# Loads of the attention layers, moved from SyncE's DMA queue to ScalarE's

## The chip, the core and the metric

The kernel runs on one core of a Trainium2 chip. The metric is the device time of one execution in microseconds (us). PE is TensorE (PEld its weight loads), DVE is VectorE, ACT is ScalarE, POOL is GpSimd and SP is SyncE. Besides computing, an engine can start DMAs: a DMA stands in the engine's instruction order like any other instruction, waits there for what it needs, is issued, and then runs on the core's 16 DMA engines by itself. SP does nothing else.

## The reference

Four graph layers over 2708 nodes with 512 features, all with the same symmetric 0/1 adjacency matrix of about 0.6% ones. Layer 2 is the one that matters here: two attention layers in a row, the second with a residual and a layer norm behind it.

```python
def _gat_layer(x, W, adj):
    proj = x @ W
    Wh, Ws = jnp.split(proj, 2, axis=-1)
    scores = Wh @ Ws.T
    a = jax.nn.softmax(scores, axis=-1) * adj
    out = a @ Wh
    out = out + x
    return jax.nn.leaky_relu(out, NEG_SLOPE)

x = _layernorm(x + _L0_gnn_ref(x, adj, deg[..., None], L0_gnn_W, L0_gnn_b), axis=-1)
x = _layernorm(x + _L1_gnn_ref(x, adj, L1_gnn_W, L1_gnn_b), axis=-1)
x = _layernorm(x + _L2_gnn_ref(x, adj, L2_gnn_W_stack), axis=-1)   # two _gat_layer
x = _layernorm(x + _L3_gnn_ref(x, adj, L3_gnn_W, L3_gnn_b), axis=-1)
```

The softmax is over all nodes, and the mask comes after it, so that every score is needed for the divisors while only the neighbours' values are summed.

## The kernel before

The nodes are cut into 22 blocks of 128 rows and, as columns, into six chunks `CH` of 512, 512, 512, 512, 384 and 276. Layers 0, 1 and 3 multiply the adjacency matrix, loaded as bytes or floats and cast by ACT to tiles `m`, into `acc` (`acc<-m,xh` and `acc<-m,xl`). The class `Attention` does the two attention layers, numbers 0 and 1.

For each attention layer the weights are first mixed (`mix`), then for each chunk the stationary side of the scores (`wst_sb`) and the values `z` are projected, and sums of quarters of the stationary side (`s1`, `s2`, `s4`, the stationary sums) are made. `keep_sums` stores these sums to DRAM, and `load_sums` brings them back when a later chunk needs them. `copy_z` copies the values into a DRAM table `pairs`.

`layer` walks over the chunks. For chunk `k` the scores of all 22 blocks against the chunk's columns are made on PE:

- `load_moving` loads the turned rows of the chunk (`xs`, four tiles), at block 15 of the chunk before.
- In chunks 0 to 3 of layer 0 and 0 to 2 of layer 1 (`SEVEN`), `pair_steps` makes two blocks at a time in seven products instead of eight: PE writes banks `spx` and `spy`, ACT copies them at once to tiles `s`, `u` and `v`, and PE adds the next product onto the same bank. In the other chunks `scores` makes each block from four products into a bank `sp`.
- `soften`, one chunk behind, takes a block of the finished chunk: DVE subtracts the column's maximum, ACT takes the exponential, DVE adds it to the divisor's sum and multiplies it by the mask `a`, and SP stores it to `pairs` (`pairs<-s`).
- `fetch`, once the whole chunk is stored, gathers the neighbours' rows of a block from `pairs` by an indirect DMA on POOL (`g<-pairs,givers`). With it come the residual rows `xr` of this and the next block (`load_rows`), and in layer 1 the first inputs `x1` (named `x<-x` in the profile).
- `weigh` multiplies the gathered rows on PE (`acc<-g`), and `end` adds the residual rows, applies the leaky relu and stores the block (`y<-r`, or after the layer norm `x<-r`).

Between these, `fill` puts in work of the next layer: the second attention layer's projections, and layer 3's first products.

The order is set by hand. The wrapper `Ordered` makes each engine run its instructions in the order of the calls:

```python
if engine in last:
    self.owner.tc.add_manual_dep(ins.ins, last[engine], ...)
last[engine] = ins.ins.name
```

`advance` keeps an estimated clock by which gathers and later steps are placed. All SBUF tiles of 2 KB a partition come from one pool of 87 pages (`page`), and a page is taken again when its last user is done. There are eight PSUM banks, in two pools of four (`bank`).

Before the change all of the loads named above, the masks and the stores stand in SP's queue; POOL's queue has the gathers and other transfers of layers 0, 1 and 3. ACT starts no DMA in the part that runs (a general path, taken for other weights only, follows it).

Of the kernel before, what the change touches and what calls it, by code (L numbers as in the profile page):

```python
# [552 lines left out]
class Fast:  # L553
# [266 lines left out]
    def load_rows(self, ly, j):  # L820
        if ly.rows[j] is None:
            ly.rows[j] = self.page(f"x{ly.number}_{j}")
            queue = self.nc.gpsimd if ly.number == 1 else self.nc.sync
            queue.dma_start(ly.rows[j], ly.source[j])
# [807 lines left out]
class Attention:  # L1632
# [414 lines left out]
    def load_sums(self, ly, k):  # L2047

        for n, name in enumerate(("s1", "s2", "s4")):
            t = self.page(f"{name}_{ly.number}_{k}", FP, (P, 2, 2 * P))  # L2050
            self.nc.sync.dma_start(t, self.sums[ly.number][k][n])
            ly.sums[k][name] = [t[:, c, :] for c in range(2)]

    def replace(self, ly, k):
# [145 lines left out]
    def load_moving(self, ch):  # L2200

        ch.xt = []
        for c in range(DC):
            t = self.page(f"xs{ch.name}_{c}")
            self.nc.sync.dma_start(
                t[:, : ch.cw], self.k.turned[ch.ly.number][ch.k][:, c, :]
            )
            ch.xt.append(t)
# [155 lines left out]
    def fetch(self, ch):  # L2364


        q, t = ch.to_fetch.pop(0)
        g = self.f.wide(f"g{ch.name}_{q}_{t}")
        i, _, w = ch.blocks[q]

        for b in (q, q + 1):
            self.load_rows(ch, b)
        if ch.ly.number == 1 and q not in ch.first:
            ch.first[q] = self.page(f"x1{ch.name}_{q}")
            self.nc.sync.dma_start(ch.first[q][:w], self.k.saved[1][i][:w])

        h = t // ONLY if t < QUARTERS * ONLY else (0, QUARTERS - 1)[q % 2]
        first, width = (P, D + (h + 1) * QW) if q % 2 else (h * QW, D + P - h * QW)
        self.nc.gpsimd.indirect_dma_start(
            out=g[:, :width],  # L2380
            out_offset=None,
            in_=ch.ly.pairs[ch.k % 2][:, :],
            in_offset=bass.IndirectOffsetOnAxis(ap=self.k.givers[:, i, t : t + 1], axis=0),
            element_offset=(q // 2) * PAIR + first,
        )

        begin = max(self.fetch_free, self.clock + (FIRST_LANDS if (q, t) == ch.first_fetch else 0))
        self.fetch_free = begin + 1.15
        ch.fetched.append((g, self.fetch_free + 6))

    def load_rows(self, ch, q):
        if q in ch.rows or q >= len(ch.blocks):
            return
        ch.rows.add(q)
        i, _, w = ch.blocks[q]
        ch.x[q] = self.page(f"xr{ch.name}_{q}")
        given = self.k.saved[1] if ch.ly.number == 0 else self.k.between
        self.nc.sync.dma_start(ch.x[q][:w], given[i][:w])

    def fetch_ahead(self):  # L2400
        count = sum(len(c.fetched) for c in self.chunks)
# [331 lines left out]
```

## Time and profile before

| | |
|---|---|
| Time, median of 3 runs | 2238.84 us |
| Lowest and highest | 2234.57 and 2247.07 us |
| The profiled execution | 2238.97 us |
| Its span, first to last instruction | 2236.7 us |
| Granted TensorE clock | 0.992 |
| First attention layer's scores | from about 735 us |
| Second attention layer's scores | from about 1420 us |
| DMA moved | 487.90 MB, 218 GB/s on average |
| SP's and POOL's queues | 36.5% and 29.3% of 16 DMA engines' span |

The profile is that of one execution. "Busy" leaves out waits, semaphores and the issue of DMAs. Rows of groups read: line, engine, operation, output<-inputs, shape, count, and then busy time or durations. Line 71 is the wrapper through which every operation is issued, so the tile names tell groups apart. In a timeline a row gives start, length, engine and operation, and in brackets how long the engine stood idle before it and what seems to have released it; "issue" means that the profile shows nothing it waited for, and "remote" an unknown queue. A wait for several things is put down to the one that came last. SPq is SP's sequencer, which issues DMAs. Times on a timeline count from the span's start.

### The profile page before, as it was taken

How to read it: one execution, taken by the hardware profiler on the slowest of the kernel's cores; microseconds unless marked ns; L12 is line 12 of the kernel's file. 1: busy time of each engine (PE TensorE's matmuls, PEld its weight loads, DVE VectorE, ACT ScalarE, POOL GpSimd, SP SyncE). 2: the span in 40 equal slices, each digit the busy share in tenths (PEclk: the TensorE clock that was granted, in tenths of full speed). 3: DMA queues.
4: the chain of work that ended last, by engine and by line, in shares of the span. 5: the costliest groups of instructions: out<-in, count | busy, mean ns of one | idle time of the engine just before them, and what ended most of it. 6: DMA issues, size and time to landing. Idle time of an engine off the chain costs nothing.

```text
span 2236.7 us, 30610 instructions
## 1 busy us (share of the span) xinstructions
PE 2182.9 (98%) x10012; PEld 1576.6 (70%) x10012; DVE 1626.8 (73%) x3425; ACT 824.9 (37%) x1855; POOL 722.2 (32%) x827
## 2 busy tenths in 40 slices
PE   9999999999999999999999999999999998999997
PEld 6777788889887888765555666788743455577896
DVE  6777888897887869987758733459979698545744
ACT  7444363333333345433323422335423223342121
POOL 2333441111000000657465452000466666643000
PEclk9999999999999999999999999999999999999999
DMA  9976762222412855999799885674899899974221
GB/s 347 287 199 171 197 189 65 88 84 91 158 58 96 289 176 155 318 327 333 244 357 342 277 287 178 212 259 134 274 324 322 284 329 354 324 242 129 94 87 43
DMA packets 310990, 487.90 MB, mean 218 GB/s; under 512 B 37434, under 2 KB 178010, under 8 KB 310820
## 3 DMA queue, kind: packets, MB, share of 16 engines
q1 hardware_dynamic: 242164, 270.69, 36.5%
q0 software_dynamic: 68656, 215.15, 29.3%
q8 instruction: 81, 1.33, 0.2%
q14 instruction: 89, 0.73, 0.1%
HBM read 356.23 MB, written 162.76 MB: 232 GB/s over the span
## 4 chain that ended last, share of the span: by engine, by line
PE 94%; DVE 2%; issue 1%; DMA 1%; another core or an unknown queue 1%; ACT 0%; DVEq 0%; ACTq 0%; POOL 0%; POOLq 0%
PE acc L71 39%; PE sp L71 13%; PE spx L71 10%; PE spy L71 7%; PE mm L71 4%; PE mmx L71 3%; PE mmy L71 2%; PE z_0x L71 2%; PE wst L71 2%; PE z_0y L71 1%; PE mix L71 1%; PE wst_0x L71 1%; PE wst_1x L71 1%; PE z_1x L71 1%; PE wst_0y L71 1%
## 5 line engine op out<-in xcount | busy, mean ns | idle before, releaser
L71 POOL DMA_INDIRECT g<-pairs,givers x510 | 540.1, 1059 | 808.0 <-DMA xr<-x 235.3
L71 PE MATMUL acc<-m,xh 128*128 128x512 f32 (+4 forms) x1584 | 562.1, 376 | 6.7 <-ACT s L71 6.7
L71 PE MATMUL acc<-m,xl 128*128 128x512 f32 (+4 forms) x1584 | 548.1, 364 | 0.3 <-issue 0.3
L71 PEld LDWEIGHTS acc<-m,xh 128*128 128x128 f32 (+1 forms) x1584 | 287.4, 188 | 64.3 <-issue 17.2
L71 PEld LDWEIGHTS acc<-m,xl 128*128 128x128 f32 (+1 forms) x1584 | 287.7, 188 | 42.4 <-issue 3.6
L71 PE MATMUL sp<-xs,wst_sb 128*128 128x384 f32 (+2 forms) x960 | 301.5, 486 | 0.1
L71 PE MATMUL acc<-g 128*32 128x512 f32 (+1 forms) x1020 | 273.1, 613 | 7.2 <-issue 4.1
L71 PEld LDWEIGHTS sp<-xs,wst_sb 128*128 128x128 f32 x960 | 166.4, 183 | 133.0 <-issue 74.4
L71 ACT CAST m<-at 128x512 fp32r<-128x512 uint8 (+5 forms) x396 | 201.8, 569 | 111.4 <-DMA at<-mask 47.9
L71 DVE TENSOR_TENSOR sum<-sum,s 128x512 f32<-128x512 f32 (+4 forms) x252 | 156.9, 623 | 30.2 <-ACT s L71 22.9
L71 DVE TENSOR_TENSOR s<-s,a 128x512 f32<-128x512 f32 (+3 forms) x264 | 166.1, 629 | 9.1
L71 PEld LDWEIGHTS acc<-g 128*32 128x32 f32 (+1 forms) x1020 | 77.9, 136 | 134.4 <-issue 105.9
L71 DVE TENSOR_TENSOR top<-top,s 128x512 f32<-128x512 f32 (+3 forms) x240 | 149.4, 623 | 26.2 <-issue 15.3
L71 DVE TENSOR_TENSOR s<-s,shift 128x512 f32<-128x512 f32 (+3 forms) x264 | 161.2, 619 | 1.6 <-issue 1.3
L71 ACT COPY s<-sp 128x384 f32<-128x384 f32 (+2 forms) x112 | 52.5, 473 | 291.3 <-PE sp L71 153.9
L71 ACT ACTIVATE s<-s 128x512 f32<-128x512 f32 (+3 forms) x264 | 146.8, 581 | 13.5 <-DVE s L71 8.4
L71 POOL DMA_DIRECT2D x<-o x44 | 25.7, 590 | 325.2 <-DVE o L71 281.8
L71 ACT COPY s<-spx 128x256 f32<-128x256 f32 x210 | 77.5, 373 | 136.7 <-PE spx L71 98.1
L71 PE MATMUL spx<-xs,wst_sb 128*128 128x256 f32 x400 | 103.2, 383 | 0.0
L71 PE MATMUL mm<-w,ht 128*128 128x512 f32 (+1 forms) x240 | 99.1, 594 | 0.0
L71 DVE SCALAR_TENSOR_TENSOR xr<-acc,rden,xr 128x512 f32<-128x512 f32 (+1 forms) x44 | 32.8, 746 | 84.6 <-PE acc L71 65.2
L71 PEld LDWEIGHTS spx<-xs,wst_sb 128*128 128x128 f32 x400 | 76.0, 191 | 19.5 <-issue 7.4
(349 smaller groups left out, 3331.0 us busy)
## 6 DMA issues: line engine op xcount, KB each, us to landing
pairs<-s SPq DMA_DIRECT2D x168, 256.0 KB
at<-in_adj_t SPq DMA_DIRECT2D x84, 256.0 KB
pairs<-pairs SPq DMA_DIRECT2D x42, 512.0 KB
s<-sums SPq DMA_DIRECT2D x60, 256.0 KB
xres<-x POOLq DMA_DIRECT2D x44, 256.0 KB
x<-o POOLq DMA_DIRECT2D x43, 256.0 KB
pairs<-z_sb SPq DMA_DIRECT2D x42, 256.0 KB
pairs<-pairs SPq DMA_DIRECT2D x42, 256.0 KB
```

The source lines that it names most:

```text
L71: ins = call(*args, **kw)
```

## The change

Four loads are issued by ACT (`nc.scalar`) instead of SP (`nc.sync`), at the same places of the program. In ACT's order they now stand between the copies and exponentials that were called before and after them. There are 60 loads of stationary sums, 40 of turned rows, 44 of residual rows and 22 of first inputs, 166 in all, of mostly 256 KB.

```diff
@@ load_sums
-            self.nc.sync.dma_start(t, self.sums[ly.number][k][n])
+            self.nc.scalar.dma_start(t, self.sums[ly.number][k][n])
@@ load_moving
-            self.nc.sync.dma_start(
+            self.nc.scalar.dma_start(
                 t[:, : ch.cw], self.k.turned[ch.ly.number][ch.k][:, c, :]
             )
@@ fetch
-            self.nc.sync.dma_start(ch.first[q][:w], self.k.saved[1][i][:w])
+            self.nc.scalar.dma_start(ch.first[q][:w], self.k.saved[1][i][:w])
@@ load_rows
-        self.nc.sync.dma_start(ch.x[q][:w], given[i][:w])
+        self.nc.scalar.dma_start(ch.x[q][:w], given[i][:w])
```

The order of PE's, DVE's and POOL's instructions stays the same, and so does that of the DMAs that are left on SP.

## The prediction

> **What bounds the kernel now.** I read the page first (busy shares and the chain that ended last):
>
> ```profile
> PE 2182.9 (98%) x10012; PEld 1576.6 (70%) x10012; DVE 1626.8 (73%) x3425; ACT 824.9 (37%) x1855; POOL 722.2 (32%) x827
> PE 94%; DVE 2%; issue 1%; DMA 1%; another core or an unknown queue 1%; ACT 0%; DVEq 0%; ACTq 0%; POOL 0%; POOLq 0%
> ```
>
> TensorE is the bound: idle for 2236.7 - 2182.9 = 53.8 us of the span, and nothing else can be won. Then the windows over the attention stages: chunks 0 to 3 of the first layer, chunks 3 to 5 of the second, and the second layer's end (columns: length, busy of PE, PEld, DVE, ACT, POOL, granted clock, DMA share, GB/s):
>
> ```profile
> 785.00:1065.00 280.00, 267.55 (x1196) 199.01 (x1194) 230.51 (x390) 115.78 (x273) 103.33 (x96) 0.98 0.78 263
> 1640.00:1890.00 250.00, 249.70 (x882) 123.50 (x881) 209.26 (x384) 78.65 (x152) 161.04 (x150) 1.00 0.94 315
> 1890.00:2005.00 115.00, 104.62 (x417) 65.90 (x416) 61.37 (x139) 49.47 (x99) 61.15 (x62) 0.97 0.88 296
> ```
>
> PE loses 12.5 us in the first and 10.4 us in the last, almost none between, where DMA is busiest. ScalarE is idle for over half of each: it has time, and what counts is when it stands still. So the timelines, first where ScalarE (ACT) paused, then the PE instruction behind it, with PE's idle time in brackets:
>
> ```profile
> 939.29 0.37 ACT L71 COPY v<-spx 128x256 f32<-128x256 f32 x1 [9.28 <-PE spx L71]
> 939.71 1.13 PE L71 MATMUL spx<-t,wst_sb 128*128 128x256 f32 x4 [0.83 <-issue]
> 955.68 0.37 ACT L71 COPY s<-spx 128x256 f32<-128x256 f32 x1 [6.96 <-remote]
> 957.60 2.07 PE L71 MATMUL spx<-t,wst_sb 128*128 128x256 f32 x4 [3.95 <-ACT v L71]
> 1062.88 0.37 ACT L71 COPY v<-spx 128x256 f32<-128x256 f32 x1 [7.39 <-issue]
> 1063.31 2.07 PE L71 MATMUL spx<-t,wst_sb 128*128 128x256 f32 x4 [4.88 <-issue]
> 1602.31 0.37 ACT L71 COPY v<-spx 128x256 f32<-128x256 f32 x1 [6.46 <-DMA pairs<-s]
> 1602.73 1.13 PE L71 MATMUL spx<-t,wst_sb 128*128 128x256 f32 x4 [0.90 <-ACT v L71]
> 1630.58 0.37 ACT L71 COPY s<-spy 128x256 f32<-128x256 f32 x1 [10.51 <-DMA pairs<-s]
> 1631.01 2.07 PE L71 MATMUL spy<-xs,wst_sb 128*128 128x256 f32 x4 [4.60 <-issue]
> ```
>
> They give a price: a pause of ScalarE costs PE the pause less 8.45, 3.01, 2.51, 5.56 and 5.91 us. I call that difference the cover; its mean is 5.1 us. Two pauses end on a store `pairs<-s`, which frees the page.
>
> **What the change removes from SP.** The rows by tile give the issues (ns: shortest, median, longest):
>
> ```profile
> L71 SPq DMA_DIRECT2D s<-sums x60: 319/404/3445, 786.2 to 1586.7; - x60
> L71 SPq DMA_DIRECT2D xs<-t x40: 319/446/946, 779.4 to 1819.2; - x40
> L71 SPq DMA_DIRECT2D xr<-x x22: 319/458/3094, 900.9 to 1344.0; - x22
> L71 SPq DMA_DIRECT2D xr<-y x22: 218/454/1049, 1583.0 to 2001.4; - x22
> L71 SPq DMA_DIRECT2D x<-x x34: 5/472/1102, 1584.0 to 2003.2; - x34
> ```
>
> Of `x<-x` only 22 are first inputs. 166 issues leave SP: 60 x 0.404 + 40 x 0.446 + 22 x (0.458 + 0.454 + 0.472) = 72.5 us. Does PE get any of it? SP mostly waits for data:
>
> ```profile
> SPq L71 <- DVE s L71: 300.1, 143, 17.4
> ```
>
> so a load ahead of a store usually delays nothing. One place shows that it can:
>
> ```profile
> 1611.52 2.02 SPq L71 DMA_DIRECT2D xs<-t  x4
> ...
> 1617.71 7.88 SPq L71 DMA_DIRECT2D pairs<-s  x3
> ```
>
> The first of these three stores had its data at 1612.8 (DVE's record) and landed at 1630.48, ending the pause of 10.51 us. With the loads gone it could go 4.9 us earlier, and the 4.60 us that PE stood go with it. I take 3 of them. Bounds: nothing, and 15.2 us if all five PE pauses above (0.83 + 3.95 + 4.88 + 0.90 + 4.60) vanish. I stay near the low end, since only two of the five name a store.
>
> [...]
>
> **What it adds to ScalarE: issue.** The same 72.5 us, if ACT needs what SP needs. No row shows ACT issuing a DMA; from the SP rows the ends are 0.32 us (53 us in all) and a stall of 3.4 us in a few of them; the median is the nearest row. Three loads take 1.3 us and four 1.8 us, under the smallest cover of 2.51 us: nothing for PE by themselves. With the cover gone, all 72.5 us.
>
> **What it adds: waits.** This is the part that decides. In the built programs every DMA of SP or ACT counts on one of eight counters, used by turns, and is made to wait until the earlier DMA on its counter has landed. On SP such a wait held up DMAs alone. On ScalarE it holds up what is queued behind it: copies that free PSUM banks (PE waits for those) and exponentials (DVE, then the stores, wait for those). For each load I took its place in ACT's order, when ACT came by there, and when the DMA it would wait for landed. At most places that had landed. The others:
>
> A. 921.60, four `xs` and an `xr` behind an exponential. The fifth waits for a store issued at 926.73 and landed at 931.46: 9.86 + 0.45 - 5.1 = 5.2 us.
> B. 942.28, the last of three `sums`: a store landed at 952.87, 10.59 us later. ACT comes 5.2 us later than before, because of A. If the store isn't put off too, 10.59 - 5.2 + 0.45 - 5.1 = 0.7 us; if it is, 5.9 us. I take 3.3.
> C. 1605.83, six loads. The fifth waits for the first, whose landing took 6.13 us: 6.13 + 2 x 0.45 - 5.1 = 1.9 us.
> D. 1620.07, until 1630.48. ACT stood there already until 1630.58: nothing.
> E. 792.11 and 798.15, 3.7 and 4.2 us, while `z` is copied. Below the cover, and SP has 7.9 us fewer loads there by then: nothing.
> F. Chunks 4 and 5 and the layers' ends: 1184.13 (8.6 us), 1278.43 (7.3), 1904.15 (11.1), 1972.85 (12.2). Beyond the cover 3.5 + 2.2 + 6.0 + 7.1 = 18.8 us; but there PE has score products in several banks or the next layer's products in hand, and the second window shows it stand for 0.3 us of 250. I take a third, 6 us; the ends are 0 and 18.8.
>
> PE and DVE's own instructions stand in the same order as before. SP's stores may now wait for a load on ACT: set beside ACT's place, each such load would have landed before SP came to the store, but for two copies of `z` (4.0 and 2.7 us late, under the cover).
>
> **Sum.** 5.2 + 3.3 + 1.9 + 6 = 16.4 us lost, 3 won: +13.4 us. The profiled execution took 2238.97 us, 2.3 us more than its span, and the median of the three runs is 2238.84: 2238.97 + 13.4 = 2252.4, say 2252 us.
>
> **Rivals.** (1) *Not slower: the stores come free.* ACT's new waits stay under the largest cover (8.45 us; A then costs 1.9 us) and the five pauses go: 15.2 - 1.9 = 13.3 us won, 2226 us. For it: the store of 1617.71 behind six loads and two others. Against: SP waiting for DVE. It decides once stores leave SP over 4.9 us earlier at most of the five pauses. (2) *Nothing shows.* Waits and wins are both inside the cover: 2239 us, give or take 8. For it: PE at 98%, and no PE stall of over 0.3 us put down to any moved load. (3) *The cover is the smallest seen*, 2.51 us, everywhere: A 7.8, B 8.5, C 4.5, E 1.6 + 2.1, F 31: 55.5 us, 2294 us. For it: the last window, where PE already loses 10.4 us in 115.
>
> **How the numbers follow.** Forecast (2243 to 2270 us) 0.50, rival 1 0.15, rival 2 0.20, rival 3 0.15. About 0.5%, 11 us, is what a measurement of this kernel can tell from no change: slower begins at 2250, faster below 2228. Of the forecast's 0.50, 0.40 lies above 2250; with rival 3 slower gets 0.55. Rival 1 gives 0.13 to faster, and the rest, 0.32, is the same. The range, 2228 to 2290, leaves out most of rival 1 and the upper part of rival 3, some 0.2; the forecast alone would be 2243 to 2270.
>
> **What would show it.** Right: in the profile after, ACT has pauses of 5 to 10 us ended by DMAs just before `xr<-x` near 922, near 942 and in the second layer's end, with PE stalls in `spx` or `acc` behind them, and PE's busy time unchanged near 2183. ACT's issues of 0.4 to 0.5 us alone, without such pauses, would mean rival 2. PE's stalls near 957, 1063 and 1631 gone, with stores earlier on SP, would mean rival 1. The prediction is wrong if PE's idle time falls, or if it grows where no load stands on ACT.

## The result, and the profile after

The changed kernel took 2272.34 us (median of 5 runs, 2263.09 to 2279.01) against 2238.84 for the kernel before (5 runs, 2234.57 to 2247.07): a ratio, over all the runs, of 1.0134, 95% interval 1.0105 to 1.0163 (the two medians alone give 1.0150). The forecast of 2252 us had the direction, and its range (2228 to 2290) holds the time, but the loss of 33.5 us is two and a half times the 13.4 us of the sum.

The profiled execution of the changed kernel took 2279.01 us (span 2277.3), the longest of its five; 40.6 us more span than before. The page after, busy shares and the chain that ended last:

```profile
PE 2195.7 (96%) x10012; PEld 1583.8 (70%) x10012; DVE 1625.9 (71%) x3425; ACT 822.6 (36%) x1855; POOL 715.1 (31%) x827
PE 86%; DVE 5%; DMA 5%; issue 2%; ACT 1%; another core or an unknown queue 1%; SPq 0%; ACTq 0%; DVEq 0%
```

PE's idle time went from 53.8 to 81.6 us, 27.8 more. The other 12.8 us are PE's own *busy* time, 2182.9 to 2195.7 for the same 10012 products: its granted clock was lower (0.992 before, 0.983 after). ACT has 2.3 us less work than before, so it is not more work that holds it up. The windows over the attention stages (length, busy of PE, PEld, DVE, ACT, POOL, granted clock, DMA share, GB/s):

```profile
780.00:1065.00 285.00, 265.89 (x1207) 200.56 (x1205) 225.87 (x386) 113.17 (x269) 92.32 (x88) 0.97 0.76 250
1065.00:1400.00 335.00, 311.84 (x1283) 193.31 (x1283) 202.02 (x421) 96.38 (x232) 174.86 (x168) 0.96 0.83 282
1640.00:1890.00 250.00, 242.94 (x842) 118.53 (x846) 204.05 (x365) 74.51 (x144) 151.38 (x144) 0.98 0.93 311
1890.00:2005.00 115.00, 101.23 (x371) 59.27 (x372) 72.28 (x156) 45.05 (x95) 64.24 (x64) 0.93 0.88 306
```

Between 1065 and 1400 PE stands for 23.2 us. In 1640 to 1890 it stands for 7.1, where it stood for 0.3 before; 4.97 of the 7.1 are one pause of the stage ahead (place C), which has moved into this window.

What ACT pays to issue (rows by tile; ns, shortest, median, longest):

```profile
L71 ACTq DMA_DIRECT2D xr<-x x22: 326/326/542, 892.6 to 1365.7; - x22
L71 ACTq DMA_DIRECT2D xr<-y x22: 301/326/444, 1602.1 to 2036.7; - x22
L71 ACTq DMA_DIRECT2D s<-sums x60: 326/337/506, 793.3 to 1609.7; - x60
L71 ACTq DMA_DIRECT2D xs<-t x40: 326/368/1452, 786.0 to 1838.7; - x40
L71 ACTq DMA_DIRECT2D x<-x x22: 301/330/1154, 1603.5 to 2037.6; - x22
```

One issue is 0.33 to 0.37 us on ACT (medians), less than SP's 0.40 to 0.47. The waits stand in the timeline. First place A, forecast for an `xr` near 922:

```profile
935.79 0.33 ACTq L71 DMA_DIRECT2D xr<-x  x1
936.15 0.37 ACT L71 COPY v<-spx 128x256 f32<-128x256 f32 x1 [13.70 <-DMA pairs<-s]
936.58 2.07 PE L71 MATMUL spx<-t,wst_sb 128*128 128x256 f32 x4 [7.43 <-ACT v L71]
```

ACT stood for 13.70 us, at the end until a store `pairs<-s` had landed; only then it issued the load, and only then made the copy that PE needed. PE's four products then took 2.07 us at a granted clock of 0.50, where four of them took 1.03 us at 928 in the trace before, at 1.00. Now the largest new pause, in the chunk loads of 1278 (before's time):

```profile
1292.20 5.46 SPq L71 DMA_DIRECT2D xt<-t  x8
...
1300.55 0.33 ACTq L71 DMA_DIRECT2D xr<-x  x1
1300.93 0.43 ACT L71 ACTIVATE s<-s 128x276 f32<-128x276 f32 x1 [11.13 <-DMA xt<-t]
1301.27 0.35 ACT L71 COPY wst_sb<-wst_0y 128x256 f32<-128x256 f32 x1
1301.94 2.07 PE L71 MATMUL wst_0x<-xt,s3mixed 128*128 128x256 f32 x4 [10.35 <-ACT wst_sb L71]
```

One `xr` load of 256 KB, whose rows DVE did not use before 1309, stood in ACT's order ahead of the four copies `wst_sb<-wst_..`. It shared its counter (number 104 in the trace) with an `xt` load that SP had issued at 1293.44 and that landed at 1300.54. ACT was at the place at 1289.80. Of the 11.13 us PE lost 10.35.

By stage, from the start of the same PE instruction in both traces (times of before; PE's idle time is counted between its instructions). The forecast's 6 us for F are split between its two stages as the parts beyond the cover, 3.5 + 2.2 to 6.0 + 7.1:

| Stage, us | Forecast | Measured | PE idle before | after |
|---|---|---|---|---|
| to 908 (E) | 0 | +0.9 | 1.4 | 1.8 |
| 908 to 1067 (A, B) | +8.5 | +7.9 | 12.5 | 18.8 |
| 1067 to 1364 (F: 1184, 1278) | +1.8 | +14.7 | 10.4 | 23.2 |
| 1364 to 1635 (C, D, the gain of 3) | -1.1 | +3.5 | 6.0 | 8.2 |
| 1635 to 1885 | 0 | +6.2 | 0.0 | 2.9 |
| 1885 to the end (F: 1904, 1973) | +4.2 | +7.0 | 10.7 | 13.6 |
| sum | +13.4 | +40.2 | 41.0 | 68.4 |

The near match of the second row is luck. Of its two places only A shows, where PE falls behind by 7.6 us. Steps of 3.0 us at 969, 4.2 at 998 and 2.2 at 1049 have no place in the sum, and 4.1 at 957 and 5.0 at 1063 are pauses of before that are gone. Nor is the last row shown to be F's. Its largest pause, in the changed kernel, names a gather:

```profile
1950.87 6.50 PE L71 MATMUL acc<-g 128*128 128x512 f32 x8 [8.49 <-DMA g<-pairs,givers]
```

In `e1_busy` (below), which moves no load, PE waits for a gather at the same product for as long (us in all, times, longest):

```profile
PE acc L71 <- DMA g<-pairs,givers: 11.7, 9, 7.9
```

### The profile page after: what moved, and what is told of

The parts are those of the page before. It is cut to its first block, busy times and chain, and to the rows that moved or that the text cites. A ratio compares the mean times of both kernels' runs of the same rounds, so it can differ in the third digit from the quotient of the medians.

```text
span 2277.3 us, 30517 instructions
## 1 busy us (share of the span) xinstructions
PE 2195.7 (96%) x10012; PEld 1583.8 (70%) x10012; DVE 1625.9 (71%) x3425; ACT 822.6 (36%) x1855; POOL 715.1 (31%) x827
## 4 chain that ended last, share of the span: by engine, by line
PE 86%; DVE 5%; DMA 5%; issue 2%; ACT 1%; another core or an unknown queue 1%; SPq 0%; ACTq 0%; DVEq 0%
PE acc L71 37%; PE sp L71 11%; PE spx L71 8%; PE spy L71 6%; PE mm L71 4%; DVE s L71 3%; PE mmx L71 3%; PE mmy L71 2%; PE z_0x L71 2%; PE wst L71 2%; PE z_0y L71 1%; PE wst_0x L71 1%; DMA pairs<-s 1%; DVE sum L71 1%; PE mix L71 1%
## 5 line engine op out<-in xcount | busy, mean ns | idle before, releaser
L71 POOL DMA_INDIRECT g<-pairs,givers x510 | 533.6, 1046 | 845.9 <-DMA wst_sb<-quarter 235.0
L71 PE MATMUL acc<-g 128*32 128x512 f32 (+1 forms) x1020 | 277.7, 624 | 12.5 <-DMA g<-pairs,givers 8.5
L71 PEld LDWEIGHTS spx<-xs,wst_sb 128*128 128x128 f32 x400 | 76.4, 192 | 19.8 <-issue 9.7
```

What stands on the lines that cost most here:

```text
L71: ins = call(*args, **kw)
```

## The experiments

They ran on other chips, where the kernel before takes 2211 us (2211.0 to 2211.6 in three sets); what carries over is the ratio to it. Theory W: ACT waits, in order, for the landing that a load needs, and holds up its copies. Rivals: I, the time that issuing takes on ACT; and S, what leaving SP's queue does to the transfers that stay there. All ratios are to the kernel before, with 95% intervals. "PE step" is by how much the start of a PE instruction moves against its predecessor, compared with the trace of `e1_busy`, whose time is that of before; the kernel before itself was not profiled on these chips.

### The change again

The edit is that of the change itself, repeated beside the others.

> The changed kernel once more, on the chip of this series, so that its parts can be compared with it: ratio to the kernel before 1.010 to 1.016 by every theory.

Measured: 2231.75 us, 1.0102 [1.0075, 1.0129]. Its waits of PE have the same names: `spx` for ACT's `v` 12.3 us, `wst_0x` for ACT's `wst_sb` 6.6 us.

### Issue time alone, and waits alone

```diff
@@ load_sums, load_moving, fetch, load_rows: behind each of the 166 loads, still on SP
+            self.stand_in()
+    def stand_in(self):
+        self.nc.scalar.copy(self.k.upto, self.k.upto)
```

> All loads stay on SP; at each of the 166 places ACT gets one small copy of a constant onto itself, about as long as the 0.33 us that a load's issue took on ACT, and waiting for nothing but ACT itself. Theory W (what costs is that ACT waits at a load for an earlier DMA to land, and that each PE pause is followed by a stretch at half clock): within 6 us of the kernel before, 2235 to 2247 us, PE's idle time as before (54 us). Rival I (ACT's time for the issue is what costs): most of the 33 us, 2260 to 2275 us.

Measured: 2211.60 us, 1.0003 [0.9989, 1.0018]. ACT had 166 more instructions of about the length of an issue and lost nothing:

```profile
L71 ACT COPY upto<-upto x166: 280/298/333, 787.0 to 1978.8; 128x128 bf16<-128x128 bf16 x166
```

Then the same copy with a wait, for the eighth transfer back in the order of the calls of SP and ACT, which is what a load would wait for (in the trace of before SP's 1224 transfers count on eight counters, 100 to 107, strictly by turns, 153 on each, and 1196 of them stand behind a wait for their own; in the changed kernel 159 of ACT's 166 loads do):

```diff
+    def stand_in(self):
+        ins = self.nc.scalar.copy(self.k.upto, self.k.upto)
+        self.k.tc.add_manual_dep(ins.ins, self.nc.hw[-9], ...)   # eight transfers back
```

> As the run with the small copies, but each copy also waits until the DMA eight transfers back (the one whose counter the load beside it uses) has landed; the loads are still on SP. Theory W: most of the loss comes back though no load has moved, 2258 to 2285 us, with ACT pauses of 5 to 13 us near 925, 945, 1285, 1610 and 1905 to 1990 us. Rival I: as the run without the wait. Rival S (it is the changed traffic, loads that go out earlier in a queue of their own): as the run without the wait, within 6 us of the kernel before.

Measured: 2226.02 us, 1.0082 [1.0060, 1.0104], with every load still on SP. The place of 1278 came back:

```profile
1277.53 0.30 ACT L71 COPY upto<-upto 128x128 bf16<-128x128 bf16 x1 [15.78 <-DMA xt<-t]
1278.75 2.08 PE L71 MATMUL wst_0x<-xt,s3mixed 128*128 128x256 f32 x4 [14.30 <-ACT wst_sb L71]
```

So I is out, as far as a copy of 0.30 us stands for an issue. The waits alone cost 0.82%, where all loads on ACT cost 1.02% (`e5_after_again`), without a single byte in another queue; that is just under the range that W gave. The totals agree better than the places. Against `e1_busy`, PE loses 1.7 us up to 1067 (before's time) and 17.6 from there to 1364 in `e2_wait`, but 12.3 and 8.8 in `e5_after_again`. So waiting alone is shown to cost at 1278; most of what the first chunks lose is not reproduced by it.

### One kind of load at a time

Residual rows and first inputs (e3), sums (e4), turned rows (e6), each alone on ACT and the others on SP:

```diff
@@ fetch, load_rows (e3_only_rows)
-            self.nc.sync.dma_start(ch.first[q][:w], ...)
+            self.nc.scalar.dma_start(ch.first[q][:w], ...)
-        self.nc.sync.dma_start(ch.x[q][:w], given[i][:w])
+        self.nc.scalar.dma_start(ch.x[q][:w], given[i][:w])
@@ load_sums (e4_only_sums)
-            self.nc.sync.dma_start(t, self.sums[ly.number][k][n])
+            self.nc.scalar.dma_start(t, self.sums[ly.number][k][n])
@@ load_moving (e6_only_xs)
-            self.nc.sync.dma_start(
+            self.nc.scalar.dma_start(
```

> Only the 44 residual rows and 22 first inputs are issued by ACT, turned rows and sums by SP. Theory W: these had the longest waits (935.79, 1300.55 and the second layer's end, with 7.4, 10.4 and 8.5 us of PE pause), so 15 to 28 us of the 33, 2254 to 2267 us. Rival I: their share of the issues, 66 of 166, 13 us, 2252 us. Rival S: their share of the bytes, about 13 us too.

> Only the 60 stationary sums are issued by ACT. Theory W: they stand only where seven products are made, and their waits were mostly short: 0 to 9 us, 2236 to 2248 us. Rival I: 60 of 166 issues, 12 us, 2251 us. Rival S: about 12 us.

> Only the 40 turned rows are issued by ACT. Theory W: their place behind an exponential had the shortest waits (0 to 4 us): ratio 0.998 to 1.004. If the parts add, the whole (1.0134) less rows (1.0066) and sums (1.0078) leaves nothing for them, -0.001. Rival S (traffic, by bytes): 40 of 166 loads, 1.003.

Measured: residual rows and first inputs 1.0066 [1.0045, 1.0087]; sums 1.0078 [1.0057, 1.0098]; turned rows 0.9952 [0.9934, 0.9971], 2201.30 us: 0.5% faster than the kernel before, and outside the 0.998 to 1.004 that I gave W. The three differences add up to +0.0096, close to the +0.0102 of all together. The rows put PE steps of 5.3 us near 943, 6.7 near 1262 and 7.1 near 1585, as W says; their total alone, 0.66%, does not tell W (0.7% or more) from I and S (0.6%). The sums cost more than the 9 us at most that W gave them.

With the turned rows on ACT two stalls of PE go or shrink (by 3.8 us near 963 and 5.7 near 1606). The first is gone in eight of the other traces too, so it says nothing of the turned rows. The second the traces explain. In `e1_busy` the four turned rows leave SP from 1585.45 on, behind stores; the store that ACT's next copy waits for follows at 1592.77, and the copy comes at 1605.33. In `e6_only_xs` the rows leave ACT from 1571.48 on, that store leaves SP at 1585.30, and the copy comes at 1596.48. PE's products around it are only 3 us earlier. PE is idle for less and busy for less:

```profile
PE 2168.1 (99%) x10012; PEld 1571.8 (71%) x10012; DVE 1625.7 (74%) x3425; ACT 825.1 (37%) x1855; POOL 721.3 (33%) x827
```

That is 32.3 us idle of a span of 2200.4, against 39.6 of 2212.6 in `e1_busy` (PE busy 2173.0).

### Off SP, but not on ACT

```diff
@@ fetch, load_rows (e7_pool_rows)
-            self.nc.sync.dma_start(ch.first[q][:w], ...)
+            self.nc.gpsimd.dma_start(ch.first[q][:w], ...)
-        self.nc.sync.dma_start(ch.x[q][:w], given[i][:w])
+        self.nc.gpsimd.dma_start(ch.x[q][:w], given[i][:w])
@@ load_moving (e11_turned_on_pool)
-            self.nc.sync.dma_start(
+            self.nc.gpsimd.dma_start(
```

> The 66 residual rows and first inputs are issued by POOL, just before the gather they belong to; ACT issues no DMA. Theory W: the loss of the run with these on ACT (1.0066) is gone, ratio 0.994 to 1.003, since no copy or exponential stands behind them. Rival S (it matters that they leave SP's queue and go out at another time): 1.005 or more, as with ACT.

> The 40 loads of turned rows in POOL's queue, all others on SP. If the gain of the turned rows on ACT (0.9952) is that they are off SP, so that stores leave SP earlier: 0.993 to 0.998 here too, with the PE stall near 1605 gone. If it is that ACT comes by the place at a better time, or if POOL's gathers are now held up: 0.999 or more.

Measured: rows on POOL 1.0003 [0.9993, 1.0013], so their loss comes with ACT's queue and not with leaving SP. Turned rows on POOL 1.0018 [1.0007, 1.0028], a miss: I expected the gain of ACT's queue again. The stall near 1606 did go (a step of -7.4 us), though that alone proves little: PE stood for 2.9 us some 20 us ahead of it, and in `e2_wait`, with every load on SP, the same stall is gone behind a pause of 3.0 us. And the gathers on POOL stood behind the loads, with new PE steps in `acc<-g` of 4.3 us near 930 and 3.4 near 1586. PE's waits for gathers rose to 17.9 us, from 11.7 in `e1_busy`:

```profile
PE acc L71 <- DMA g<-pairs,givers: 17.9, 14, 5.1
```

### Waits at one kind of place

The waiting copy of `e2_wait`, at one of the four places, loads on SP:

```diff
@@ load_sums (e9_wait_sums)
             self.nc.sync.dma_start(t, self.sums[ly.number][k][n])
+            self.stand_in()
@@ load_moving (e10_wait_turned)
                 t[:, : ch.cw], self.k.turned[ch.ly.number][ch.k][:, c, :]
             )
+            self.stand_in()
```

> All loads on SP as before. At the 60 places of the stationary sums alone, ACT does one in-place copy of 128x128 and waits there until the eighth transfer back has landed. W (ACT's wait is the loss): close to the loads of sums on ACT, 1.005 to 1.010, with a PE step of some 10 us near 943. If the sums cost for another reason (their issue time, or their place in the queue of ACT's own transfers): 0.999 to 1.002, no step there.

> The same waiting copy at the 40 places of the turned rows alone, loads on SP. W: at these places the transfer eight back has mostly landed, so 0.999 to 1.003. If the waits there cost too, and the gain of the turned rows on ACT only hides it: 1.004 or more.

Measured: waits at the turned rows 0.9999 [0.9988, 1.0010], in W's range but not for W's reason. The transfer eight back had often not landed: at 13 of the 40 places ACT stood for a store `pairs<-s`, 24.6 us in all and 7.8 at most. PE lost nothing by it. Waits at the sums 1.0016 [1.0005, 1.0027], a fifth of what the sums on ACT cost: a miss for W. The step near 946 is there (8.7 us; the sums on ACT have 10.2 near 943), and in both kernels 5.4 us of the shift are made up by 981. What the waits do not bring is a second step, of 6.3 us, that the sums on ACT have near 1000. In `e4_only_sums`:

```profile
1000.80 0.59 SPq L71 DMA_DIRECT2D pairs<-s  x1
1000.86 0.35 ACTq L71 DMA_DIRECT2D s<-sums  x1
1001.31 0.89 ACTq L71 DMA_DIRECT2D s<-sums  x2
...
1011.86 0.37 ACT L71 COPY s<-spy 128x256 f32<-128x256 f32 x1 [6.28 <-DMA pairs<-s]
1012.28 2.08 PE L71 MATMUL spy<-xs,s 128*128 128x256 f32 x4 [5.43 <-ACT s L71]
```

The store of 1000.80 took 11.0 us to land, and ACT's copy into its page waited for it. In `e1_busy` the same store, with the same three loads *behind* it in SP's queue, took 7.3 us, in `e9_wait_sums` 6.9, and in `e5_after_again`, with the loads in ACT's queue beside it, 12.5. Another store, of 935.74 in `e4_only_sums`, took 17.4 us against 12.5. My reading is that a load taken out of the store's queue no longer stands behind it but takes DMA time from it. No run isolates it, and it is argued, not shown.

### The best of both, tried and failed

Turned rows on ACT, the other three kinds on POOL, to have none of them behind SP's stores:

```diff
@@ load_moving
-            self.nc.sync.dma_start(
+            self.nc.scalar.dma_start(
@@ load_sums, fetch, load_rows
-            self.nc.sync.dma_start(...)
+            self.nc.gpsimd.dma_start(...)
```

> Turned rows on ACT; sums, residual rows and first inputs on POOL; none of the four on SP. W with the neutral move of rows to POOL: as good as turned rows on ACT alone, 0.992 to 0.997. If POOL's gathers then wait behind the sums: 1.000 or more, with PE waiting at acc for g.

Measured: 2244.94 us, 1.0150 [1.0123, 1.0177]. The sums came too late behind POOL's gathers:

```profile
PE spy L71 <- DMA s<-sums: 33.0, 3, 15.8
```

What is left as the best is the turned rows alone on ACT.

### What a pause of PE costs beside itself

```diff
@@ ten pauses put into PE's stream in an earlier layer
+        if ly.number == 1 and k < 5 and g in (1, 2):
+            self.stand(24 if g == 1 else 6)
+    def stand(self, n):       # two transposes; between them n copies in a chain on ACT
```

> Apart from the change: the kernel before with ten pauses of PE in layer 1, where nothing else stops it: PE turns a constant, ACT copies it 24 times (five places) or 6 times (five places) onto itself, one copy waiting for the other, and PE turns the result. Theory W with the clock: after each long pause (about 8 us) and each short one (about 2 us) PE's granted clock is 0.5 for 3 to 10 us, and the time grows by the pauses plus half of those stretches: 50 us of pauses and some 10 to 30 us on top. Without an effect on the clock: the pauses alone, and a granted clock of 1.00 in every window after them.

Measured: 2295.47 us, 1.0378 [1.0349, 1.0407], by the medians 83.9 us more. In the profiled execution PE stood for 62.6 us at the ten places. Its span is 77.8 us above that of `e1_busy`: 58.0 of idle time (other pauses became shorter) and 19.8 of busy time (2192.8 us). Of the 19.8 the twenty transposes fill 2.3 us in which PE had nothing else to do. PE worked 45.3 us at half clock, and 13.6 in `e1_busy`; half of the difference, 15.9 us, is what the clock took. Waits of PE, and windows (granted clock third from the end) through a pause of 10.26 us that ended at 385.1 and one of 2.00 that ended at 396.6:

```profile
PE stand L71 <- ACT stand L71: 62.6, 10, 10.3
```

```profile
374.00:384.00 10.00, 0.83 (x5) 0.43 (x3) 9.48 (x16) 8.61 (x26) 0.00 (x0) 0.70 0.01 1
384.00:388.00 4.00, 2.90 (x8) 2.33 (x9) 3.60 (x5) 3.03 (x8) 0.00 (x0) 0.50 0.13 46
388.00:394.00 6.00, 6.00 (x28) 4.78 (x26) 0.00 (x0) 0.00 (x0) 0.00 (x0) 0.98 0.00 0
397.00:404.00 7.00, 7.00 (x32) 5.78 (x31) 6.52 (x23) 1.19 (x3) 2.33 (x4) 1.00 0.38 152
```

After the long pause PE worked at half its clock until 388; after the short one the clock stayed whole. Each of the five long pauses (8.0 to 10.3 us) had such a stretch, and both pauses of 4.0 us a shorter one; of the three pauses of 2.0 us one had.

## Why the prediction was right in its direction, and wrong in its size

**Right: the mechanism.** ACT waits in order for a landing that the load needs, and holds the copies behind it; issue time is hidden. Both were shown apart: 1.0003 for the time, 1.0082 for the waits alone. The place of each wait was found from the trace of before: A (5.2 us forecast, a stall of 7.43 and a step of 7.6), C (1.9; a step of 5.1), 1278 (a wait of 7.3; 11.13), 1904 (a wait of 11.1; ACT stood for 10.34, but PE's pause there names a gather). Waiting is not the whole of the loss, though: the sums on ACT cost five times what waits at their places cost. "ACT's issues of 0.4 to 0.5 us" were 0.33 to 0.37.

**Wrong: the third of F.** The step that failed most is "I take a third, 6 us", for the waits where "PE has score products in several banks or the next layer's products in hand". At 1278 that left 0.7 us, a third of 7.3 - 5.1; PE lost 10.35. The wait was longer, 11.13 us, and the product in hand was `wst_0x`, which needs the bank that ACT's copy `wst_sb<-wst_0x` empties, and that copy stood behind the load. PE's cover there was 11.13 - 10.35 = 0.8 us, not 5.1, and in `e2_wait` 15.78 - 14.30 = 1.5. I had read "0.3 us of 250" off a window (1640 to 1890) that holds none of the four places of F. Where ACT stood for over 5 us in it, up to 12.65 before 1744.90, the trace of before puts that down to PE's own products: ACT waited for PE, which shows no cover. The stage with 1184 and 1278 lost 14.7 us, where I had 1.8. Another 4.0 of the 14.7, at 1217, stand behind a pause of ACT that no load on ACT ended, and none of the later traces has them.

**Wrong: one cover for all places.** The mean of 5.1 us came from five pauses, all of them in chunks with `spx` and `spy`. After the change it was 13.70 - 7.43 = 6.3 us at A and 0.8 at 1278. My range took in the smallest *seen*, 2.51; the smallest there *is* was outside it.

**Wrong: a term left out.** "PE's busy time unchanged near 2183" did not hold: it rose by 12.8 us, 32% of what the span gained. In the stretches of half clock PE worked 24.1 us before and 49.2 after; half of the difference is 12.6 us, nearly all of the rise. So PE's idle time is not all that can be won or lost: with the turned rows alone on ACT its busy time fell by 4.9 us against `e1_busy`. The clock, in windows through the pause of 10.35 us:

```profile
1296.00:1300.00 4.00, 0.00 (x0) 0.00 (x0) 0.00 (x0) 0.00 (x0) 0.71 (x1) 0.50 0.95 331
1302.00:1312.00 10.00, 10.00 (x33) 6.65 (x34) 3.65 (x7) 2.44 (x7) 1.90 (x2) 0.74 0.64 202
1312.00:1318.00 6.00, 6.00 (x27) 4.25 (x25) 3.43 (x8) 1.70 (x4) 4.76 (x5) 1.00 0.95 324
```

The first row has no work and half a clock already; the second works at 0.74 on average; from 1312 it is whole again. The trace of before had the sign of it in lines that I quoted: 2.07 us for four products after pauses of 3.95, 4.88 and 4.60 us, 1.13 after 0.83 and 0.90. I read the brackets and not the durations.

**B was hidden in the changed kernel.** I had 3.3 us for the last of three `sums` near 942. After the change PE worked through from 946 to 956 without a pause; with the sums alone on ACT the same place costs 10.2 us. That fits the one of my two cases in which ACT, late after A, finds the store nearly landed (0.7 us); no run tests it.

**Rival 1: real for the turned rows, not shown in the changed kernel.** Three of the five pauses of before (957, 1063, 1631) are gone after the change, 4.1 + 5.0 + 4.8 us where I had won 3. Two of these are gone in `e1_busy` as well, which changes nothing for SP but ran on another chip. That leaves 1631, and there the changed kernel has a new pause of 4.97 us shortly ahead (at 1613), which gives the store time to land; in `e2_wait`, with all loads on SP, the same pause is gone behind a new one too. Turned rows alone on ACT show the gain by itself: 0.9952. Waits at their places cost PE nothing (0.9999), and a store leaves SP earlier. In POOL's queue the same loads gained nothing (1.0018). The move to ACT paid for these 40 loads and not for the other 126 (rows 1.0066, sums 1.0078).

**Rivals 2 and 3.** Nothing shows: out. The cover as small as 2.51 everywhere: too pessimistic at B and E, too optimistic at 1278.

**What stays open.** Why the sums on ACT cost 1.0078 when waits at their places cost 1.0016: the slower landing of stores beside them is read from two stores, and not tested. Why the waits alone come near the whole loss (1.0082 of 1.0102) with their losses at other places. That waits of the rows' places alone would account for the rows in full (1.0082 less the 0.0016 and -0.0001 of the other two kinds leaves 1.0067, against 1.0066 measured) is a subtraction, not a run. What the last stage's 7.0 us are: in `e5_after_again` PE made up 3.4 us there against `e1_busy`. Of the 6.2 us between 1635 and 1885, 3.9 are a pause of 1.95 us near 1843, for which the profile names no releaser, and the half clock behind it; the rest is spread.

## What to carry to other kernels

A DMA on ACT cost its issue time here (0.33 us, hidden: copies of 0.30 us in its place gave 1.0003) *and* everything that it had to wait for, its completion counter's previous transfer included (11.13 us at 1278), paid by the instructions behind it. Move a load to a compute engine only if, at its place, that transfer has landed, or if the bound engine has work in hand for as long as the wait; otherwise an idle engine is not a free queue. To price such a wait, look at how much work the bound engine has ahead of the next product that the waiting engine feeds: 0.8 us at 1278, where the wait counted almost in full, 6.3 at A. A pause of PE of 4 us or more cost another 1.6 to 3.0 us here by the clock.

## What the runs showed of the hardware

- PE's granted clock fell to 0.50 during a pause, or soon after it (0.8 us behind the pause of 2.02 us that ended at 1064.07 in the changed kernel), and stayed there into the work behind it. In the traces the stretches of half clock come in multiples of 3.4 us, but for the last, which the end of the trace cuts off. In `e8_stand` pauses of 8.0 to 10.3 us brought stretches of 10.2 to 13.7 us, which began 2.6 to 5.0 us into the pause and lasted 3.1 to 6.1 us into the work; two pauses of 4.0 us brought 3.4 and 6.8 us, three of 2.0 us one of 3.4. Half of the time worked at half clock was lost (four products took 2.07 us instead of 1.03), 1.6 to 3.0 us with each long pause. A pause of 2.0 us was enough in one of the three cases in `e8_stand`, and before 1064.07 in the changed kernel.
- The same loads stood differently by the queue they were in: the sums behind POOL's gathers, in `e12_split`, came up to 15.8 us too late for PE; with the sums on SP, in `e1_busy`, no wait of PE ends on them.
